# Output weights of an attention layer: both halves of a block made at once, differences written to memory instead of in place

## The chip, the cores and the metric

The kernel runs on one core of a Trainium2 chip. The metric is the time of one execution on the device in microseconds (us); lower is better. A core has a matrix engine (TensorE, "PE" in the profile, with its weight loads as "PEld"), a vector engine (VectorE, "DVE"), a scalar engine (ScalarE, "ACT"), GpSimd ("POOL") and SyncE ("SP"), which here issues all DMAs. Each engine works through its own queue in order and waits for the others by semaphores. Matmul results land in PSUM, in banks of 128 x 512 float32; only TensorE, VectorE and ScalarE work there. The other on-chip memory is SBUF.

## The reference, cut to what matters

Four residual blocks on x of shape 4 x 512 x 1024, each behind a layer norm: a small attention, a linear layer with routed low-rank additions, a causal attention with 32 heads over a compressed key/value of width 64, and a second linear layer with low-rank additions. The change lies in the causal attention, at its end:

```python
kv = _rmsnorm(ckv, kv_a_ln_w) @ wkv_b.T            # per head: 64 columns of keys, 128 of values
...
attn = jax.nn.softmax(scores, axis=-1)
out = jnp.einsum('bhqk,bkhd->bqhd', attn, v).reshape(B, S, H * VD)
return out @ wo.T
```

The kernel never makes v. A head's value weights (64 x 128) and its rows of `wo` (128 x 1024) are multiplied beforehand into a 64 x 1024 output weight; two heads make one 128 x 1024 block. The attention's result stays in the compressed form (64 numbers a head and token) and is multiplied by these blocks.

## The kernel before, in words

**Units.** The causal attention runs over 4 groups of 8 heads, and in each group over 4 batches: 128 units (group, batch, head), in the loop at L1215. In iteration u the kernel issues the scores of unit u (`scores`, four matmul groups of 512, 384, 256 and 128 columns into the two banks `pss`; VectorE masks each at L919, ScalarE takes the exponential at L922), the transposes of unit u-1 (`turn`, ten 128 x 128 transposes into the two banks `pst` at L943, copied at L945 by ScalarE twice and VectorE once), the context of units u-3 and u-2 together every second time (`context`, L959, the bank `psv`), and the query of unit u+3 (`query`, one bank `psq`, copied by ScalarE at L729, rotated by VectorE at L731 and L732 and by POOL at L733 and L734). `split_query` makes the high and the low part of a query for the scores: the cast `qh` on VectorE (L741), then the difference `ql` on POOL (L742).

Matmuls in full precision are three matmuls of split operands: each operand is a high part (a rounded copy) plus a low part (the difference to it). Lines L150, L151 and L152 (`matmul3`) carry these; their order is low x high, high x low, high x high, so `ql` is needed first. Transposes, contexts and the blocks below are single float32 matmuls.

**Fillers.** Between these, each iteration takes some steps from a generator, the filler, in three places; `per` (L1222) says how many in each. For most of the time the filler is `project`: the product of a batch's context with the group's output weights, seven products in place of eight for each 2 x 2 of blocks, into the banks `poa` and `pob`, added into x by VectorE (L1036). For the first batch of a group it is `prepare_output` (L1052): for group 0 over eight units, for groups 1 to 3 over the last four units of that batch. The order in which a scheduler then puts the instructions on each engine is fixed when the program is built; it may move a filler's instructions past those of the units around it.

**prepare_output.** Seven weights are wanted from a 2 x 2 of blocks, b11 and b12 (the halves, columns 0 to 511 and 512 to 1023, of one head pair), b21 and b22 (those of another): b11, b21 and b22 themselves, and t1 = b12 - b11, t2 = b22 - t1, t3 = b22 - b12, t4 = b21 - t2. A group has two such sets, and each of the 14 weights is kept as a high and a low part (tiles of the pool `wup`, one buffer each). `block` (L1063) makes one half of a block by two matmuls (L1069) into `poa` or `pob`, from `slotC`, the one buffer into which SyncE loads the weights of a head pair (L1047, L1049); after the second half the next pair is fetched. `kept` (L1077) copies a bank to `room`, six places of 128 x 512 in SBUF (named `raw` in the profile), on ScalarE. `high` (L1080) casts on ScalarE. `low` (L1086) subtracts on VectorE if its source is a bank, on POOL if it is a place of `room`. `less` (L1094) is a difference of two sources: on POOL if all is in `room`, otherwise on VectorE. Before, t1, t2 and t4 are made in the bank in which an operand stands, and t3 in `room` by POOL. One bank at a time is filled and worked off, so that 18 of the 32 half blocks stand alone among TensorE's instructions and 14 as pairs.

`kept`, `high`, `low` and `less` are 24 operations on ScalarE, 16 on VectorE and 6 on POOL in a group. VectorE's are held behind the last mask by `issue_after`.

## Time and profile before

| | |
|---|---|
| median of 3 runs | 1743.06 us (1740.99 to 1744.13) |
| the profiled execution | 1745.28 us |
| its span, first to last instruction | 1743.1 us |
| mean granted clock of TensorE | 0.998 |
| stages with output weights (us of the span) | 443 to 501, 739 to 776, 1010 to 1047, 1281 to 1318 |

The profile is of one execution. Busy times are sums over an engine's instructions; a busy TensorE is not TensorE at its peak, since the ends of pipelined matmuls are modelled. A row of a timeline has the start, the time from the first start to the last end of equal instructions in a row, the engine, the line, the operation with output<-input and shapes, the count, and in brackets the idle time before it with what ended it. A row of a group has minimum, median and maximum of one instruction in ns. A row of the waits has who waited for whom, the sum in us, how often, and the longest. The stages of groups 1 to 3 are alike; one of them in the table by stage:

```profile
739.00:776.00 37.00, 36.67 (x204) 23.55 (x200) 30.25 (x78) 29.76 (x78) 22.70 (x20) 1.00 0.59 194
```

Its columns are the stretch, its length, the busy time and count of PE, PEld, DVE, ACT and POOL, the granted clock, the share of the DMA engines and GB/s.

### The profile page before, as it was taken

Reading aid. Unit: us, or ns where it says so; the run is one execution under the profiler, and the core shown is the slowest. Engines: PE = TensorE matmul, PEld = TensorE weight load, DVE = VectorE, ACT = ScalarE, POOL = GpSimd, SP = SyncE. Lnnn points to the kernel's source line nnn. Section 1 sums busy time; section 2 is a strip of 40 time slices with the busy share of each in tenths; the row PEclk is TensorE's granted clock in tenths of the full one; section 3 lists DMA queues with packets and bytes.
Section 4 is the critical chain, followed back from the end, with each engine's and each line's share of the span. In section 5 each row is a group of like instructions: output and inputs, shape, how many; then the busy total and the mean of one; then the engine's idle time right before and its main releaser. Section 6 shows DMA issues by size and latency. Waiting matters only on the chain.

```text
span 1743.1 us, 31732 instructions
## 1 busy us (share of the span) xinstructions
PE 1703.5 (98%) x10536; PEld 1431.2 (82%) x10536; DVE 1305.5 (75%) x3494; ACT 902.6 (52%) x2316; POOL 925.4 (53%) x926
## 2 busy tenths in 40 slices
PE   7999999999999999999999999999999999999999
PEld 6899999998667877767787767777767777789998
DVE  7977885677877777787777777777778776687675
ACT  7422331366765555475555476555476555453332
POOL 0553541203666664666666656666566664575454
PEclk9999999999999999999999999999999999999999
DMA  4313543245324234353333353342454333853331
GB/s 195 134 40 118 181 164 114 89 139 164 115 87 150 81 109 150 104 176 114 110 122 113 105 201 97 105 140 95 133 168 151 103 111 120 303 196 122 138 117 62
DMA packets 131940, 228.17 MB, mean 131 GB/s; under 512 B 22272, under 2 KB 58752, under 8 KB 128448
## 3 DMA queue, kind: packets, MB, share of 16 engines
q1 hardware_dynamic: 131776, 226.13, 38.4%
q8 instruction: 84, 1.38, 0.3%
q14 instruction: 80, 0.66, 0.1%
HBM read 156.60 MB, written 71.83 MB: 131 GB/s over the span
## 4 chain that ended last, share of the span: by engine, by line
PE 85%; DVE 6%; DMA 3%; ACT 2%; issue 2%; POOL 2%; SPq 0%; ACTq 0%; DVEq 0%; POOLq 0%
PE psv L959 8%; PE pst L943 7%; PE po L150 4%; PE po L152 4%; PE po L151 4%; PE pss L150 4%; PE pss L151 4%; PE pss L152 3%; PE pob L150 3%; PE psq L150 3%; PE psq L151 3%; PE psq L152 3%; PE poa L150 3%; PE acc L150 3%; PE acc L152 3%; PE acc L151 3%
## 5 line engine op out<-in xcount | busy, mean ns | idle before, releaser
L922 ACT ACTIVATE p<-p,mn 128x512 f32<-128x512 f32 (+3 forms) x512 | 284.7, 558 | 218.0 <-DVE mn L919 217.6
L919 DVE CUSTOM_DVE_ANT_0 p<-pss,causal 128x512 f32<-128x512 f32 (+3 forms) x512 | 232.4, 486 | 27.4 <-PE pss L152 21.8
L733 POOL TENSOR_TENSOR qf<-qf,ropeT 64x512 f32<-64x512 f32 x128 | 164.6, 1286 | 166.4 <-ACT qf L729 163.4
L943 PE MATMUL pst<-ident,p 128*128 128x128 f32 x1280 | 186.4, 274 | 4.0 <-ACT pT L945 4.0
L734 POOL TENSOR_TENSOR qf<-qf,wA 64x512 f32<-64x512 f32 x128 | 164.4, 1285 | 29.9 <-DVE wA L732 23.4
L943 PEld LDWEIGHTS pst<-ident,p 128*128 128x128 f32 x1280 | 153.4, 141 | 31.4 <-ACT pT L945 8.7
L742 POOL TENSOR_TENSOR ql<-qf,qh 128x384 fp32r<-128x384 f32 x128 | 131.1, 1024 | 62.9 <-DVE qh L741 44.3
L994 POOL TENSOR_TENSOR cxl<-s,cxh 128x256 fp32r<-128x256 f32 x128 | 96.5, 762 | 120.6 <-ACT cxh L993 66.9
L945 ACT COPY pT<-pst 128x512 f32<-128x512 f32 x256 | 142.2, 577 | 23.2 <-PE pst L943 21.6
L150 PE MATMUL pss<-kT,ql 128*128 128x512 f32 (+2 forms) x384 | 142.8, 372 | 0.5 <-POOL ql L742 0.2
L150 PE MATMUL po<-w_h,hTl 128*128 128x384 f32 (+1 forms) x384 | 133.0, 346 | 0.5 <-DVE x L433 0.5
L151 PE MATMUL pss<-kT,qh 128*128 128x512 f32 (+2 forms) x384 | 130.9, 341 | 0.0
L152 PE MATMUL po<-w_h,hTh 128*128 128x384 f32 (+1 forms) x384 | 130.1, 339 | 0.0
L152 PE MATMUL pss<-kT,qh 128*128 128x512 f32 (+2 forms) x384 | 129.8, 338 | 0.0
L151 PE MATMUL po<-w_l,hTh 128*128 128x384 f32 (+1 forms) x384 | 129.7, 338 | 0.0
L945 DVE COPY pT<-pst 128x256 f32<-128x256 f32 x128 | 54.3, 424 | 94.2 <-PE pst L943 93.1
L729 ACT COPY qf<-psq 128x512 f32<-128x512 f32 x126 | 73.8, 586 | 71.9 <-PE psq L152 71.8
L731 DVE TENSOR_TENSOR wA<-psq,ropeT 32x512 f32<-32x512 f32 x126 | 87.7, 696 | 22.4 <-ACT qf L729 19.5
L994 POOL TENSOR_TENSOR cxl<-cx,cxh 128x256 fp32r<-128x256 f32 x96 | 73.5, 767 | 56.1 <-ACT cxh L993 53.5
L922 ACT ACTIVATION_READ_ACCUMULATOR p<-p,mn 128x1 f32 x512 | 97.0, 189 | 0.0
L150 PEld LDWEIGHTS pss<-kT,ql 128*128 128x128 f32 x384 | 72.1, 188 | 20.9 <-issue 3.6
L732 DVE TENSOR_TENSOR wA<-psq,ropeT 32x512 f32<-32x512 f32 x126 | 87.1, 691 | 1.7
(511 smaller groups left out, 4976.9 us busy)
## 6 DMA issues: line engine op xcount, KB each, us to landing
xs<-x_d SPq DMA_DIRECT2D x128, 256.0 KB
x_d<-xs SPq DMA_DIRECT2D x128, 256.0 KB
slotC<-in_woT_dram SPq DMA_DIRECT2D x32, 512.0 KB
rb<-r_d SPq DMA_DIRECT2D x128, 128.0 KB
w_t<-raw SPq DMA_DIRECT2D x32, 288.0 KB
x<-in_x_dram SPq DMA_DIRECT2D x16, 512.0 KB
x_d<-x SPq DMA_DIRECT2D x32, 256.0 KB
slotA<-q_d SPq DMA_DIRECT2D x8, 1024.0 KB
```

What stands on the lines that cost most here:

```text
L150: T.matmul(ps, lhsT=al, rhs=bh, start=start, stop=False, **kw)
L151: T.matmul(ps, lhsT=ah, rhs=bl, start=False, stop=False, **kw)
L152: T.matmul(ps, lhsT=ah, rhs=bh, start=False, stop=stop, **kw)
L733: G.tensor_tensor(f[mid], f[mid], ropeT[mid, 0, :], ALU.mult)
L734: G.tensor_tensor(f[mid], f[mid], t2[mid], ALU.add)
L742: G.tensor_tensor(l, f[:, P:S], f32(h), ALU.subtract)
L919: turn_of[0] = V.tensor_tensor_reduce(out=to, in0=ps[:, 0:n], in1=causal[:, S - n : S], scale=1.0, scalar=-NEG, op0=ALU.add, op1=ALU.min, ...
L922: A.activation(to, to, AF.Exp, bias=mn[:, i : i + 1], scale=-1.0, accum_out=rs[:, i : i + 1])
L943: T.transpose(ps[:, w : w + P], p[:, OF[i] + j * P : OF[i] + (j + 1) * P], ident)
L945: copy(pT[:, AT[js[0]] : AT[js[0]] + w], ps[:, 0:w])
L959: T.matmul(ps[n * KVR : (n + 1) * KVR, S - w : S], lhsT=k[:, j, :], rhs=pTs[u + n][:, AT[j] : AT[j] + w], start=(j == 0), stop=(j == TPB - 1))
L994: G.tensor_tensor(l, src, f32(h), ALU.subtract)
```

## The change

`block` now makes both halves, `poa` and `pob`, one right after the other, and fetches the next head pair behind them. Only b12 and b22 are copied to `room`; t1, t2, t3 and t4 are all made by VectorE from one operand in a bank and one in `room` (t3 from b22's bank and the kept b12), and written to places of `room`. So their high parts are cast from `room`, and their low parts, like that of b22, are made by POOL. A group has 18 operations on ScalarE, 12 on VectorE and 10 on POOL. There are 24 steps a group, the same for both sets, and `per` hands them out evenly: one in each of the three places for group 0, two in each for the other groups. The core of the diff:

```diff
-            def block(n, half, at):
+            def block(n):
                 nonlocal fetched
                 wo, wv = fetched
-                po[at] = pso.tile([P, 512], F32, name="po" + at)
                 with ExitStack() if g else tc.issue_after(scored[0].ins):
-                    for k in range(2):
-                        T.matmul(po[at][k * KVR : (k + 1) * KVR, :], lhsT=wv[:, k, :],
-                                 rhs=wo[k][:, half * 512 : half * 512 + 512], start=True, stop=True)
-                if half and n + 1 < len(prs):
+                    for half, at in enumerate("ab"):
+                        po[at] = pso.tile([P, 512], F32, name="po" + at)
+                        for k in range(2):
+                            T.matmul(po[at][k * KVR : (k + 1) * KVR, :], lhsT=wv[:, k, :],
+                                     rhs=wo[k][:, half * 512 : half * 512 + 512], start=True, stop=True)
+                if n + 1 < len(prs):
                     fetched = fetch_output(g, prs[n + 1])
...
             def less(to, a0, a1):
-                if not {to, a0, a1} & set(po):
+                if not {a0, a1} & set(po):
...
             def steps():
...
+                for n in (0, 2):
+                    block(n)
+                    if n:
+                        low("t4", 2)
+                    yield
+                    kept(1, "b")
+                    high("b11", "a")
+                    yield
+                    less(4, 1, "a")
+                    low("b11", "a")
+                    yield
+                    high("t1", 4)
+                    yield
+                    low("t1", 4)
+                    yield
+                    yield
+                    block(n + 1)
+                    yield
+                    kept(3, "b")
+                    high("b21", "a")
+                    less(5, "b", 4)
+                    yield
+                    high("b22", 3)
+                    low("b21", "a")
+                    less(2, "a", 5)
+                    less(0, "b", 1)
+                    yield
+                    high("t2", 5)
+                    low("b22", 3)
+                    yield
+                    high("t3", 0)
+                    low("t2", 5)
+                    yield
+                    high("t4", 2)
+                    low("t3", 0)
+                    if n:
+                        low("t4", 2)
+                    yield
...
-            per = ((4, 1, 0) if i % 2 else (1, 1, 0)) if b else (2 + (i < HG // 2 + 2), 2, 2) if i >= HG // 2 else (3, 3, 1)
+            per = ((4, 1, 0) if i % 2 else (1, 1, 0)) if b else (2, 2, 2) if i >= HG // 2 else (3, 3, 1)
             if B == 0:
-                per = (0, 1, 2)
+                per = (1, 1, 1)
```

The steps that went are the 22 written out one by one at L1101 to L1177.

More of the change, by code (lines that the diff above doesn't have):

```diff
@@ L1101, in steps @@
             def steps():
-                block(0, 0, "a")
-                yield
-                kept(0, "a")
-                high("b11", "a")
-                block(0, 1, "b")
-                yield
-                low("b11", "a")
-                kept(1, "b")
-                yield
-                less("b", "b", 0)
-                block(1, 0, "a")
-                yield
-                high("t1", "b")
-                kept(0, "b")
-                kept(2, "a")
-                high("b21", "a")
@@ L1118, in steps @@
-                yield
-                low("t1", "b")
-                low("b21", "a")
-                block(1, 1, "b")
-                yield
-                high("b22", "b")
-                kept(3, "b")
-                yield
-                low("b22", 3)
-                less("b", "b", 0)
-                block(2, 0, "a")
-                yield
-                high("t2", "b")
-                kept(5, "a")
-                less(3, 3, 1)
-                yield
-                low("t2", "b")
@@ L1135, in steps @@
-                less("b", 2, "b")
-                high("b11", "a")
-                yield
-                high("t4", "b")
-                high("t3", 3)
-                low("b11", "a")
-                yield
-                low("t4", "b")
-                low("t3", 3)
-                block(2, 1, "a")
-                yield
-                kept(1, "a")
-                yield
-                less("a", "a", 5)
-                block(3, 0, "b")
-                yield
-                high("t1", "a")
@@ L1152, in steps @@
-                kept(5, "a")
-                kept(2, "b")
-                high("b21", "b")
-                yield
-                low("t1", "a")
-                low("b21", "b")
-                block(3, 1, "a")
-                yield
-                high("b22", "a")
-                kept(3, "a")
-                yield
-                low("b22", 3)
-                less("a", "a", 5)
-                yield
-                high("t2", "a")
-                less(3, 3, 1)
-                yield
@@ L1169, in steps @@
-                low("t2", "a")
-                less("a", 2, "a")
-                high("t3", 3)
-                yield
-                high("t4", "a")
-                low("t3", 3)
-                yield
-                low("t4", "a")
-                yield
+                for n in (0, 2):
[36 more added lines that the diff above has]
+                    yield
```

## The prediction, made before the result was known

> **What bounds the kernel now.** I read the page first, then TensorE's waits, then the timelines of the four stretches in which the output weights are prepared (443 to 501 us for group 0; 739 to 776, 1010 to 1047 and 1281 to 1318 us for groups 1 to 3).

> ```profile
> PE 1703.5 (98%) x10536; PEld 1431.2 (82%) x10536; DVE 1305.5 (75%) x3494; ACT 902.6 (52%) x2316; POOL 925.4 (53%) x926
> ...
> PE 85%; DVE 6%; DMA 3%; ACT 2%; issue 2%; POOL 2%; SPq 0%; ACTq 0%; DVEq 0%; POOLq 0%
> ```

> TensorE is busy 98% of the span and holds 85% of the chain that ends last. So work taken from VectorE (DVE), ScalarE (ACT) or POOL is worth only what TensorE waits for it, and TensorE's own order counts. Over the whole span its second-largest wait is this one:

> ```profile
> PE pst L943 <- ACT pT L945: 4.0, 5, 2.2
> ```

> 2.2 of the 4.0 us are one wait near the end of group 0's preparation; three others of 0.49 us close the preparations of groups 1 to 3. The timeline shows what stands behind the long one:

> ```profile
> 487.82 0.39 PE L150 MATMUL pss<-kT,ql 128*128 128x512 f32 x1
> 490.46 0.44 PE L943 MATMUL pst<-ident,p 128*128 128x128 f32 x2 [2.25 <-ACT pT L945]
> ...
> 491.89 1.91 PE L943 MATMUL pst<-ident,p 128*128 128x128 f32 x8
> ...
> 502.59 1.04 PE L943 MATMUL pst<-ident,p 128*128 128x128 f32 x8
> ```
> ```profile
> 484.06 0.59 ACT L1083 CAST t21h<-poa 128x512 fp32r<-128x512 f32 x1 [1.51 <-DVE poa L1099]
> 487.13 0.62 ACT L1083 CAST t31h<-raw 128x512 fp32r<-128x512 f32 x1 [2.48 <-POOL raw L1096]
> ...
> 489.84 1.04 ACT L945 COPY pT<-pst 128x512 f32<-128x512 f32 x2
> ```
> ```profile
> 481.72 1.30 POOL L733 TENSOR_TENSOR qf<-qf,ropeT 64x512 f32<-64x512 f32 x1 [1.73 <-ACT qf L729]
> 483.09 1.28 POOL L1089 TENSOR_TENSOR b221l<-raw,b221h 128x512 fp32r<-128x512 f32 x1
> 484.45 1.28 POOL L734 TENSOR_TENSOR qf<-qf,wA 64x512 f32<-64x512 f32 x1
> 485.81 1.28 POOL L1096 TENSOR_TENSOR raw<-raw 128x512 f32<-128x512 f32 x1
> ```

> ScalarE stands still for t3, whose difference POOL makes (L1096). Behind the standing cast wait four exponentials and then the copies of the transposes (L945), and TensorE waits for these: 2.25 us. After it the eight transposes take 1.91 us where they normally take 1.04: the granted clock is 0.5 for one stretch of 3.41 us, from 491.5 (the 0.97 mean clock in the table by stage for 443 to 501). That costs about 1.7 us more.

> **The change part by part.**

> *Engine work.* Per group ScalarE loses 6 copies (24 in four groups, 0.48 us from start to start: 11.5 us), VectorE 4 operations (16, 0.60 us: 9.6 us), POOL gains 4 (16, 1.36 us from start to start by the rows above: 21.8 us). All of it lies beside TensorE's work: 0 by itself.

> *TensorE's blocks.* The matmuls are the same 64; only their neighbours change. A lone block, and a pair behind a context stage (psv):

> ```profile
> 445.74 0.39 PE L152 MATMUL psq<-slotA,wqh 128*128 128x512 f32 x1
> 446.06 1.08 PE L1069 MATMUL pob<-slotC 128*64 128x512 f32 x4
> 447.07 0.44 PE L943 MATMUL pst<-ident,p 128*128 128x128 f32 x2
> 447.26 0.48 PE L150 MATMUL pss<-kT,ql 128*128 128x512 f32 x1
> ...
> 1279.35 2.38 PE L959 MATMUL psv<-pT,slotA 128*64 128x512 f32 x16
> 1281.56 1.03 PE L1069 MATMUL poa<-slotC 128*64 128x512 f32 x4
> 1282.42 1.03 PE L1069 MATMUL pob<-slotC 128*64 128x512 f32 x4
> 1283.37 0.39 PE L150 MATMUL pss<-kT,ql 128*128 128x256 f32 x1
> ```

> From the psq row to the pss row it is 1.52 us with the block and 0.37 without it (459.92 to 460.29): 1.15. Other lone blocks come to 1.11 to 1.22; I take 1.17. Context stage and pair take 4.02 us; a context stage alone takes 2.30 (439.51 to 441.81): the pair costs 1.72. Before, 18 half blocks stand alone and 7 pairs together (pairs inside a context stage cost 1.7 to 1.9): 18 x 1.17 + 7 x 1.75 = 33.3. In the built order of the changed program there are 16 pairs: 10 behind a context stage (1.72) and 6 in the middle of other work, where each also pays about 0.1 on both sides (2.0): 29.2. **-4.1 us**; bounds -2.6 (lone blocks no dearer than 1.09) and -4.7.

> *Waits that go.* No high part waits for POOL any more. 2.25 + 1.7 + 3 x 0.49 = 5.4 us. Before, the second load of slotC arrived 0.23 and 0.29 us late in two groups, since only two steps lay between a fetch and its block; now there are six: 0.5. **-5.9 us.** Next in line ScalarE waits for VectorE's differences (0.6 us each, in the same queue as the masks); TensorE has transposes, a query and scores (3 us) to do before it needs ScalarE again, and that hides them. Without this cover it would be 0.6 a difference, at most 1.2 a place.

> *The burst on POOL.* Lows of t1, t2 and t4 move to POOL, and the built order puts them in a row: in group 0, after each second block, rotation L733, low t2, low t3, rotation L734, low t4, and only then the low part ql of the query that the next unit's scores need first. Nothing of before does this; there ql came right behind its own rotation. I add it up from the start of such a block, by rows of before:
> - TensorE: block 1.82, scores 0.46, last scores 0.22, eight transposes 0.80, query 1.48: 4.77. The result of the query is there at 5.03.
> - ScalarE copies it, POOL starts L733 0.72 us later: 5.75. Five operations at 1.36: ql starts at 12.55, ends (1.02) at 13.6.
> - TensorE meanwhile, from 4.77: two transposes 0.14, scores of 512 columns 0.78 (447.26 to 448.04), of 384 0.62, four transposes 0.44, one context matmul 0.43: 7.2. The next query waits for VectorE's rotation (L731, L732: ScalarE's copy, then two of 0.70 behind a difference) until 7.4. Query 1.5, four transposes and the short scores, with the waits for VectorE's masks between them, 2.9 in all: at 10.3 TensorE needs ql.

> A stall of 3.3 us, in two places of group 0. Nothing hides it. Bounds for one: 0 (if the scheduler's neighbours give POOL its copy 3.3 us earlier) and 4.7 (one more 1.36). As 2.25 us of idle time took half a clock stretch before, I add 1.7 each: 2 x 5.0 = **+10.0 us**.

> [...]

> *The same burst in groups 1 to 3.* Units there are longer (9 us for 7). Middle: ql is ready 12.4 us after the block's start, TensorE comes at 12.45: a tie. End: four lows stand between L733 and L734, so the cast of the next query (L741) holds VectorE until 9.4, the mask of the next scores ends at 12.05 and TensorE comes at 11.9; VectorE then runs about 0.4 late once more. I take 0.6 a group: **+1.8 us**; bounds 0, and 8.2 if each of the six places is one POOL operation (1.36) later. The table by source shows that the cast suffers from a busy POOL as it is:

> ```profile
> L741 DVE CAST qh<-qf x128: 310/362/740, 418.5 to 1462.2; 128x384 fp32r<-128x384 f32 x128
> ```

> [...]

> *Sum.* -4.1 - 5.9 + 10.0 + 1.8 = +1.8 us. The profiled execution took 1745.28 us (span 1743.1), 2.2 above the median of the runs, 1743.06. On the median: **1744.8 us**, no change that a measurement of this kernel can tell (about 0.2%, 3.5 us).

> **Rivals.**
> - *The burst is hidden* (the query's copy comes earlier, or TensorE later by work I did not see): only the gains stay, -10.0, or -8.2 with the ties: 1733 to 1735. For it: POOL is busy 37.5 of 58 us in group 0, so on average there is room. Against it: the order is fixed, and five times 1.36 behind one copy is more than the 5.3 us that TensorE has left.
> - *The burst also stalls groups 1 to 3* (the other side). Same mechanism: ql and the cast behind L734. Price 1.36 a place, six places: 8.2 in place of 1.8: 1751. It decides from 0.2 us of lateness on, since both places are ties. [...] Against it: groups 1 to 3 show 0.5 us or less of any such wait now.
> - *Half of the new stalls*: one of the two places hidden: 1740.
> - That the change does not do what it says is excluded: the built order shows 18, 12 and 10 operations a group.

> **How the numbers follow.** Forecast 0.50 (its own range 1740 to 1749: 0.05 faster, 0.37 same, 0.08 slower), burst hidden 0.17 (0.16 faster, 0.01 same), groups 1 to 3 too 0.25 (0.24 slower, 0.01 same), half 0.08 (0.05 faster, 0.03 same). Faster 0.26, same 0.42, slower 0.32. The range takes in most of both sides: 1733 to 1753.

> **What would show it.** Right: no wait of ScalarE for POOL; 16 pairs of blocks; TensorE waiting for "POOL ql L742" twice between 443 and 505 us, about 3 us each, with two clock stretches of 0.5; no waits above 0.5 us in groups 1 to 3. Wrong: ql on time (then about 1734), or waits for ql or for the mask in every group (then 1750 and more).

## The result, and the profile after

The changed kernel takes 1747.97 us (median of 7 runs, 1745.68 to 1754.8), the kernel before, beside it on the same chip, 1743.06 (7 runs, 1740.88 to 1744.55): a ratio of 1.0035, 95% interval 1.0023 to 1.0046. It is slower by 4.9 us. The forecast was 1744.8 in a range of 1733 to 1753. The time lies in the range, but beyond the bound of 0.2% within which the forecast called it no change. The profiled execution took 1746.9 us, its span is 1744.7. Of the executions below, one of run 6 (5862.85 us) and one of run 10 (2095.26 us) lie far above all others; the ratios leave them out, the medians count them.

The page's first line and its chain, after. TensorE is as busy as before, ScalarE 8.5 us less (11.5 reckoned), VectorE 7.1 less (9.6) and POOL 22.6 more (21.8); POOL's share of the chain has doubled (4% for 2%):

```profile
PE 1702.5 (98%) x10536; PEld 1433.1 (82%) x10536; DVE 1298.4 (74%) x3478; ACT 894.1 (51%) x2292; POOL 948.0 (54%) x942
...
PE 85%; DVE 5%; POOL 4%; ACT 3%; issue 2%; DMA 1%; SPq 0%; POOLq 0%; ACTq 0%; DVEq 0%
```

Two of TensorE's waits, after (who waited for whom, sum in us, times, longest). The first was 0.2 us before, the second 2.9, and the wait for ScalarE's copies (4.0) has shrunk to 0.3:

```profile
PE pss L150 <- POOL ql L742: 5.4, 3, 2.6
PE pob L150 <- POOL cxl L994: 4.9, 5, 1.6
```

TensorE's timeline has the two stalls at the two predicted places, 2.61 us each, and after the second one the rest of a context stage that takes 3.98 us for 14 records, at half clock (0.57 granted from 500 to 504 us, 0.50 from 500.09 to 503.50). (A float32 matmul of a context or a block stands in the profile as two records, so that a context stage of eight matmuls has 16.) The first row is the scores right behind the block of the first place:

```profile
455.67 0.39 PE L150 MATMUL pss<-kT,ql 128*128 128x256 f32 x1
...
464.49 0.38 PE L943 MATMUL pst<-ident,p 128*128 128x128 f32 x2
467.48 0.50 PE L150 MATMUL pss<-kT,ql 128*128 128x512 f32 x1 [2.61 <-POOL ql L742]
...
498.77 0.50 PE L150 MATMUL pss<-kT,ql 128*128 128x512 f32 x1 [2.61 <-POOL ql L742]
...
500.22 3.98 PE L959 MATMUL psv<-pT,slotB 128*64 128x512 f32 x14
```

POOL's timeline ahead of the first stall is the chain of the prediction (the difference of a low part is now L1090), without a break from 459.59 on. TensorE has its `ql` at 467.48, 11.81 us after the scores behind the block (455.67). Predicted were 13.6 from the block's start, 1.82 of them for the block, so 11.8 from there. The block itself is mixed with the last matmuls of a context here, from 453.21 on:

```profile
459.59 1.28 POOL L733 TENSOR_TENSOR qf<-qf,ropeT 64x512 f32<-64x512 f32 x1 [1.21 <-ACT qf L729]
460.96 1.28 POOL L1090 TENSOR_TENSOR t20l<-raw,t20h 128x512 fp32r<-128x512 f32 x1
462.19 1.41 POOL L1090 TENSOR_TENSOR t30l<-raw,t30h 128x512 fp32r<-128x512 f32 x1
463.68 1.28 POOL L734 TENSOR_TENSOR qf<-qf,wA 64x512 f32<-64x512 f32 x1
465.04 1.44 POOL L1090 TENSOR_TENSOR t40l<-raw,t40h 128x512 fp32r<-128x512 f32 x1
466.44 1.95 POOL L742 TENSOR_TENSOR ql<-qf,qh 128x384 fp32r<-128x384 f32 x2
```

One thing in TensorE's order was not reckoned with. Four of the five context stages in group 0's preparation now have their first matmul (two records) issued early and alone; from 446.99 to the next start it is 1.00 us, and as much at 460.59:

```profile
446.99 1.07 PE L959 MATMUL psv<-pT,slotA 128*64 128x512 f32 x2
447.99 0.38 PE L150 MATMUL pss<-kT,ql 128*128 128x256 f32 x1
```

Where the time went, by TensorE's starts: from the 512-column scores of unit 3 to those of unit 13 (group 0's preparation), and of units 38 to 50 (group 1's). A matmul's time is that to the next start; idle time over 0.06 us is kept apart.

```
units 3 to 13     blocks  contexts  queries  projection  scores, transposes  idle   total
before              7.49     14.38    14.96        5.16               31.30  2.25   75.53
after               8.04     15.94    15.27        5.12               30.51  5.44   80.31
units 38 to 50
before              7.25     15.04    17.77       22.31               35.66  1.00   99.04
after               8.24     14.89    17.46       21.93               35.50  1.02   99.04
```

Group 0 is 4.8 us longer; group 1 is equal to 0.01, group 2 0.24 longer, group 3 0.22 shorter. So between these two executions the change costs time in group 0 alone, and about as much as the medians differ (4.9). Each kernel has one profiled execution, and half clock falls otherwise in others (mean clocks from 0.995 to 1.000, last section). The two spans differ by only 1.6, since the execution profiled before had a half-clock stretch near its start (at 51.2 us; the later one was 1.88 us ahead at unit 0) and lost 1.4 more from the last unit's scores on; both are outside the stages that the change touches.

### The profile page after: what moved, and what is told of

It reads as the page before. It is cut to its first block, busy times and chain, and to the rows that moved or that the text cites. A ratio compares the mean times of both kernels' runs of the same rounds, so it can differ in the third digit from the quotient of the medians.

```text
span 1744.7 us, 31689 instructions
## 1 busy us (share of the span) xinstructions
PE 1702.5 (98%) x10536; PEld 1433.1 (82%) x10536; DVE 1298.4 (74%) x3478; ACT 894.1 (51%) x2292; POOL 948.0 (54%) x942
## 4 chain that ended last, share of the span: by engine, by line
PE 85%; DVE 5%; POOL 4%; ACT 3%; issue 2%; DMA 1%; SPq 0%; POOLq 0%; ACTq 0%; DVEq 0%
PE psv L959 8%; PE pst L943 7%; PE po L150 4%; PE po L152 4%; PE po L151 4%; PE pss L150 4%; PE pss L151 3%; PE pss L152 3%; PE pob L150 3%; PE poa L150 3%; PE psq L150 3%; PE psq L151 3%; PE psq L152 3%; PE pob L152 3%; PE pob L151 3%; PE acc L150 3%
## 5 line engine op out<-in xcount | busy, mean ns | idle before, releaser
L733 POOL TENSOR_TENSOR qf<-qf,ropeT 64x512 f32<-64x512 f32 x128 | 164.5, 1285 | 159.6 <-ACT qf L729 157.6
L943 PE MATMUL pst<-ident,p 128*128 128x128 f32 x1280 | 183.7, 273 | 0.3 <-ACT pT L945 0.3
L734 POOL TENSOR_TENSOR qf<-qf,wA 64x512 f32<-64x512 f32 x128 | 164.7, 1287 | 25.9 <-DVE wA L732 18.8
L943 PEld LDWEIGHTS pst<-ident,p 128*128 128x128 f32 x1280 | 152.2, 141 | 27.3 <-ACT pT L945 5.4
L742 POOL TENSOR_TENSOR ql<-qf,qh 128x384 fp32r<-128x384 f32 x128 | 131.7, 1030 | 61.1 <-DVE rt L884 24.6
L945 ACT COPY pT<-pst 128x512 f32<-128x512 f32 x256 | 141.8, 577 | 43.0 <-PE pst L943 42.0
L994 POOL TENSOR_TENSOR cxl<-s,cxh 128x256 fp32r<-128x256 f32 x128 | 96.9, 764 | 119.7 <-ACT cxh L993 68.4
L150 PE MATMUL pss<-kT,ql 128*128 128x512 f32 (+2 forms) x384 | 142.3, 370 | 6.0 <-POOL ql L742 5.4
L150 PE MATMUL po<-w_h,hTl 128*128 128x384 f32 (+1 forms) x384 | 132.9, 346 | 0.0
L152 PE MATMUL po<-w_h,hTh 128*128 128x384 f32 (+1 forms) x384 | 130.1, 339 | 0.0
L152 PE MATMUL pss<-kT,qh 128*128 128x512 f32 (+2 forms) x384 | 129.4, 337 | 0.0
L945 DVE COPY pT<-pst 128x256 f32<-128x256 f32 x128 | 54.2, 424 | 94.3 <-PE pst L943 93.6
L729 ACT COPY qf<-psq 128x512 f32<-128x512 f32 x126 | 73.5, 584 | 71.0 <-PE psq L152 70.7
L994 POOL TENSOR_TENSOR cxl<-cx,cxh 128x256 fp32r<-128x256 f32 x96 | 73.1, 763 | 58.2 <-ACT cxh L993 55.5
L731 DVE TENSOR_TENSOR wA<-psq,ropeT 32x512 f32<-32x512 f32 x126 | 87.7, 696 | 22.0 <-ACT qf L729 19.1
L150 PEld LDWEIGHTS pss<-kT,ql 128*128 128x128 f32 x384 | 72.2, 188 | 29.5 <-issue 7.3
L732 DVE TENSOR_TENSOR wA<-psq,ropeT 32x512 f32<-32x512 f32 x126 | 87.1, 691 | 1.7
```

The costliest lines, as they stand in the source:

```text
L150: T.matmul(ps, lhsT=al, rhs=bh, start=start, stop=False, **kw)
L152: T.matmul(ps, lhsT=ah, rhs=bh, start=False, stop=stop, **kw)
L733: G.tensor_tensor(f[mid], f[mid], ropeT[mid, 0, :], ALU.mult)
L734: G.tensor_tensor(f[mid], f[mid], t2[mid], ALU.add)
L742: G.tensor_tensor(l, f[:, P:S], f32(h), ALU.subtract)
L943: T.transpose(ps[:, w : w + P], p[:, OF[i] + j * P : OF[i] + (j + 1) * P], ident)
```

## The experiments

Theory 1 is the prediction's: the burst of low parts on POOL makes `ql` late in group 0, and that costs two stalls and clock. Theory 2, the rival: TensorE's new order costs the time, by the context matmuls that are issued alone. Theory 3: half-clock stretches that fall by chance. Ten kernels were run, each timed against the kernel before, which had medians of 1743.1, 1742.9 and 1742.7 us in the three sets.

**1. `ql` ahead of the low parts.** `split_query` keeps its difference, and `low` queues POOL's low parts behind it; TensorE's, VectorE's and ScalarE's orders are unchanged:

```diff
-        G.tensor_tensor(l, f[:, P:S], f32(h), ALU.subtract)
+        split_of[0] = G.tensor_tensor(l, f[:, P:S], f32(h), ALU.subtract)
...
-                    G.tensor_tensor(l, src(at), f32(h), ALU.subtract)
+                    with tc.issue_after(split_of[0].ins):
+                        G.tensor_tensor(l, src(at), f32(h), ALU.subtract)
```

> The changed kernel with the low parts on POOL queued behind the query's low part (ql) that was split last; TensorE's, VectorE's and ScalarE's orders are those of the changed kernel, instruction by instruction. Theory 1 (the burst on POOL makes ql late): both waits of 2.61 us for ql in group 0 go, with the clock stretch (1.7 us) that one of them took: 5.2 to 6.9 us less than the changed kernel, 1741 to 1743. Theory 2 (the new order of TensorE costs the time: context stages whose first two matmuls are issued alone, about 1.0 us each): its order is unchanged, so the time stays at 1747 to 1748. Theory 3 (the difference is clock stretches that fall by chance in the runs): no difference from the changed kernel outside the interval.

Measured: 1743.23 us, 4.7 less than the changed kernel; against before 1.000 (0.9991 to 1.0008). First POOL, then TensorE at the same place: `ql` now goes ahead of the low parts, and TensorE passes from the transposes to the scores without a wait.

```profile
461.52 1.27 POOL L734 TENSOR_TENSOR qf<-qf,wA 64x512 f32<-64x512 f32 x1 [0.22 <-DVE wA L732]
463.16 1.00 POOL L742 TENSOR_TENSOR ql<-qf,qh 128x384 fp32r<-128x384 f32 x1 [0.36 <-DVE qh L741]
464.12 1.30 POOL L1093 TENSOR_TENSOR b220l<-raw,b220h 128x512 fp32r<-128x512 f32 x1
```
```profile
465.06 0.38 PE L945 MATMUL pst<-ident,p 128*128 128x128 f32 x2
465.19 0.48 PE L150 MATMUL pss<-kT,ql 128*128 128x512 f32 x1
```

Group 0 takes 74.06 us in place of 80.31: the burst cost 6.25. The stalls (5.2) and the half clock behind the second (contexts 14.33 for 15.94) are gone, and 1.0 of smaller waits has come. Theory 1 holds for the difference between the kernels; theories 2 and 3 would have left the time where it was.

**2. A longer burst** (b22's low part three times in group 0):

```diff
-                    G.tensor_tensor(l, src(at), f32(h), ALU.subtract)
+                    for _ in range(3 if g == 0 and kind == "b22" else 1):
+                        G.tensor_tensor(l, src(at), f32(h), ALU.subtract)
```

> The changed kernel with the low part of b22 in group 0 made three times instead of once, so that two more POOL operations (2.6 us) stand ahead of each of the two bursts; all other engines have the same order. POOL stands still for 1.21 us there, so its chain is 1.4 us later. Theory 1: each of the two waits for ql grows from 2.6 to 4.0 us: 2.8 us more than the changed kernel, 4.5 if the longer idle time takes one more clock stretch: 1750.5 to 1752.5. Theories 2 and 3: no change (1747 to 1748).

Measured: 1754.36 us, 6.4 more than the changed kernel, above what theory 1 expected. Each stall is 3.83 us, 1.22 longer (1.4 expected), and now both are followed by half clock (0.57 granted from 470 to 474 us and from 504 to 508). The matmul behind the first:

```profile
470.12 0.68 PE L150 MATMUL pss<-kT,ql 128*128 128x512 f32 x1 [3.83 <-POOL ql L742]
```

In the traces group 0 grows by 4.4: 2.9 of idle time, 2.4 of it in the two stalls, and 1.4 of clock. The two profiled executions differ by 5.7 in all, 1.2 of it ahead of unit 0. So the cost follows the length of the burst, as theory 1 has it; theories 2 and 3 had no change.

**3. Context stages in one piece**, in all groups; `last_of[0]` is the last matmul of the latest scores that have their low parts, those of 384 columns when a context is issued:

```diff
+            with tc.issue_after(last_of[0].ins):
+                for j in range(TPB):
...
+                        T.matmul(ps[n * KVR : (n + 1) * KVR, S - w : S], lhsT=k[:, j, :],
```

> The changed kernel with each context stage queued behind the scores of 384 columns of its own iteration, so that no first pair of context matmuls is issued alone; in the new order 7 pairs of blocks stand behind a context stage and 9 behind a query, where 10 and 6 stood behind a context stage and behind scores. Theory 2: four split stages in group 0 and two to three in each of the other groups give back about 1.0 us each, 10 to 12 us, less 3 x 0.3 for the pairs that no longer follow a context stage: 1737 to 1739. Theory 1: in group 0 TensorE only comes earlier to the same late ql, so that half of what is saved there is given back in the two waits (about 3.6 us each instead of 2.6): 2 us less gain, 1739 to 1741, with both waits for ql still there and longer. Theory 3: no difference.

Measured: 1754.3 us, 6.3 more than the changed kernel, where no theory expected more time. Theory 2 falls as it was stated. In group 0 the context matmuls go down (13.45 us for 15.94), but both waits for `ql` stay (2.82 and 2.71 us), each is followed by half clock, and the first half-clock stretch is a double one (the context stage behind it, 16 records in one piece, takes 4.26 us). In groups 1 to 3 the edit did not do what it was meant to: no first matmul is alone, but two stages a group are now split elsewhere, around transposes, and in units 38 to 50 contexts take what they took (14.87 us for 14.89) and TensorE's own time is no less (98.42 for 98.02). So this run does not test theory 2 there. Idle time grows in each of these groups (1.75, 1.75 and 2.92 us for 1.02, 1.02 and 0.82). One of these two stages:

```profile
756.55 2.15 PE L961 MATMUL psv<-pT,slotA 128*64 128x512 f32 x10
758.63 0.66 PE L944 MATMUL pst<-ident,p 128*128 128x128 f32 x4
759.22 0.86 PE L961 MATMUL psv<-pT,slotA 128*64 128x256 f32 x6
```

**4. Both edits.**

> Both edits together: context stages in one piece, and the low parts on POOL behind the query's low part. Theories 1 and 2 together: no wait for ql, no lone pairs: 1747.5 - 6 - 10 = 1731 to 1734, faster than the kernel before. Theory 1 alone: as the first of these runs, 1741 to 1743. Theory 2 alone: as the third, 1737 to 1739.

Measured: 1746.24 us; 1.0016 (1.0008 to 1.0025), outside all three expectations. With both edits group 0 is 1.2 us shorter than in the first run (72.85 for 74.06), and groups 1 to 3 are 0.9, 0.9 and 2.4 longer. TensorE's waits in this run:

```profile
PE pob L150 <- DVE xs L1040: 3.6, 4, 1.3
...
PE pst L946 <- ACT pT L948: 2.3, 4, 0.7
```

The projection waits for VectorE's sums, and the transposes for ScalarE's copies. It looks as if the lone matmuls had filled time in which these were made; that was not tried by itself, and in groups 1 to 3 two stages are split around transposes as in run 3.

**5. The kernel before, with ScalarE's cast of t3 behind the exponentials.** Nothing of the change is in it:

```diff
-                A.copy(h, src(at))
+                with tc.issue_after(exp_of[0].ins) if kind == "t3" else ExitStack():
+                    A.copy(h, src(at))
```

> The kernel before with one edit: ScalarE's cast of t3 is queued behind the exponentials of its iteration, so that ScalarE no longer stands still for POOL's difference in front of them. Nothing of the change itself is in it. If the prediction's term for the wait that goes is right (2.25 us, a clock stretch of 1.7, 0.49 in each of three groups), 5.4 us less than before: 1737 to 1739. If the wait is filled by the next one in line (VectorE's differences, or ql), 1741 to 1743.

Measured: 1737.98 us; 0.9972 (0.9963 to 0.9981). ScalarE's copies of the transposes come in time, and the cast stands behind them:

```profile
487.62 0.57 ACT L946 COPY pT<-pst 128x512 f32<-128x512 f32 x1
488.13 0.59 ACT L729 COPY qf<-psq 128x512 f32<-128x512 f32 x1
488.62 0.62 ACT L1085 CAST t31h<-raw 128x512 fp32r<-128x512 f32 x1
```

4.9 us of the 5.4 expected are there. In group 0 it is 4.3 (71.22 us for 75.53). Idle time is 1.7 of it (0.51 for 2.25), and the 3.41 us at half clock are worth another 1.7. The remaining 0.9 is about what run 6 gives for a context stage in one piece (0.8): one that was split there before (at 493.73) is whole now. VectorE's and POOL's built orders have shifted a little with the edit too. Groups 1 to 3 change by -0.3, +0.1 and -0.3, where 1.5 was reckoned: their waits for ScalarE, 0.5 at most, are still there. This kernel beats both.

**6. The first run's kernel, with the contexts of group 0 alone in one piece** (the `issue_after` of run 3 under `if g == 0`).

> The first experiment's kernel (low parts on POOL behind ql) with the context stages of group 0 alone kept in one piece; those of the other groups stay as in the changed kernel, and so do all pairs of blocks. If a context stage whose first two matmuls are issued alone costs about 0.5 us (2.1 us between the first and the fourth run in group 0, for four stages), 2 us less than the first run's 1743.2: 1741. If what was gained there came from the shifted pairs of blocks instead, no change (1743).

Measured: 1742.14 us; 0.9995 (0.9986 to 1.0004), 1.1 less than the first run. The contexts of group 0 take 11.12 us in place of 14.33, 0.8 less for each of the four stages, which are whole now:

```profile
452.61 2.38 PE L963 MATMUL psv<-pT,slotA 128*64 128x512 f32 x16
```

But the idle time rises from 1.23 to 3.01 (waits for masks, for VectorE's sums and for ScalarE), and the stage is 1.2 shorter, about half of what was expected.

**7. The low parts of the last t3 and t4 of groups 1 to 3 on VectorE**, the rest as in the first run:

```diff
+                    if g and len(wouts[g][kind]) == 2 and kind in ("t3", "t4",):
+                        with tc.issue_after(turn_of[0].ins):
+                            V.tensor_tensor(l, src(at), f32(h), ALU.subtract)
+                        return
```

> The first experiment's kernel with the low parts of the last t3 and t4 of groups 1 to 3 on VectorE instead of POOL, two POOL operations less in the burst of four at the end of each of these stages. If that burst is what makes TensorE wait for the projection's low part (L994) at the stage's end, 1.02, 1.01 and 0.82 us in the three groups, these go: 2 to 2.8 us less than 1743.2: 1740.5 to 1741.2. If VectorE's two more operations delay masks by as much, no change.

Measured: 1745.09 us; 1.0015 (1.0006 to 1.0024), 1.9 more than the first run, which neither side expected. At the stages' ends the waits for the projection's low part shrink from 1.02, 1.01 and 0.82 us to 0.2 or nothing, and waits for masks come (0.7, 0.7 and 1.5). The whole execution's rows for these two:

```profile
PE pss L150 <- DVE mn L921: 3.4, 6, 0.8
...
PE pob L150 <- POOL cxl L996: 2.0, 2, 1.6
```

So whichever of POOL and VectorE gets the operations is late. But that is not the whole of the loss: in groups 1 and 2 idle time is as before the edit (1.09 and 1.07 us for 1.02 and 1.01), and the stages are 1.1 and 0.9 longer by TensorE's own contexts, queries and projection, whose order has changed too.

**8. The halves of a block in different steps again**, the rest as in the first run: `block(n, 1)`, a step, `block(n, 0)`, with the work on a bank behind its own half.

> The first experiment's kernel with the two halves of a block made in different steps again; in its order 12 half blocks stand alone, the others in pairs or fours, where the changed kernel has 16 pairs. By the prediction's prices (1.17 us a lone half, 1.72 to 2.0 a pair) 12 x 1.17 + 10 x 1.75 + 0.7 = 32.2 in place of 29.2: 3 us more, 1746. If a half block costs the same alone as in a pair, as the sums over a stage of the kernel before and of the first run say (blocks, contexts, queries and projection of units 38 to 50: 62.4 us before, 62.5 after), no change: 1743.

Measured: 1751.06 us; 1.0045 (1.0032 to 1.0059). Slower by 7.8 than the first run, and above both expected numbers. In units 38 to 50 blocks, contexts, queries and projection take 7.10 + 16.04 + 17.44 + 21.92 = 62.50 us, where the first run has 8.17 + 14.96 + 17.46 + 21.93 = 62.52, and the kernel before, with its 18 lone halves in all, 62.37. The masks are late:

```profile
PE pss L150 <- DVE mn L921: 4.3, 2, 3.3
PE pss L915 <- DVE mn L921: 3.2, 4, 1.0
```

In the new steps one has four operations of VectorE; that these are what delays the masks is read from the order and was not tried. The longest of the waits, 3.28 us, is followed by half clock too (the two 384-column matmuls that come next take 0.53 us each, those at 438.88 in the trace before 0.34 and 0.35). The disputed price of a half block is not settled by the equal sums: the three kernels split their context stages in different places (blocks 8.17 and contexts 14.96 us in the first run, 7.10 and 16.04 here), and a split costs about as much as the price in question (0.8 us, run 6).

**9. Run 5 with all context stages in one piece.**

> The fifth experiment's kernel (the kernel before, ScalarE's cast of t3 behind the exponentials) with every context stage in one piece too. Three context stages there, one in each of groups 1 to 3, have their first two matmuls issued alone. If these cost 0.5 to 0.8 us each and nothing takes their place, 1.5 to 2.4 us less than 1738.0: 1736. If the wait for copies or masks takes their place, as in the third experiment's groups 1 to 3 (1 to 2 us a group more), 1738 to 1742.

Measured: 1738.0 us; 0.9974 (0.9964 to 0.9984), the same as run 5. Group 0 is 1.0 shorter. In groups 1 to 3 contexts lose 1.3 us each, and a wait of 1.5 for the low part of t4 comes in their place.

**10. One part of the change undone, in group 0 alone: the low parts of t2, t3 and t4 on VectorE.**

```diff
+                    if g == 0 and kind in ("t2", "t3", "t4"):
+                        with tc.issue_after(turn_of[0].ins):
+                            V.tensor_tensor(l, src(at), f32(h), ALU.subtract)
+                        return
```

> The changed kernel with one part of the change undone in group 0 alone: the low parts of t2, t3 and t4 are made by VectorE (held behind the last mask) instead of POOL. Theory 1 (POOL's burst): both waits for ql go with the clock stretch, 1741 to 1743, as in the first experiment. If VectorE's three more operations (0.6 us each) make a mask late by what is taken from POOL, a wait for masks takes their place: 1745 and more.

Measured: 1743.25 us; 1.0004 (0.9995 to 1.0013). No wait for `ql` and no half clock in group 0 (the mean clock of the profiled execution is 1.000); what comes in place is one wait of 1.2 us for VectorE's copy and 0.8 of smaller ones. Two different ways of taking the burst off POOL's path (1 and 10) give the same time.

## Why the prediction was in the range and on the wrong side of no change

The way from before to after in group 0 falls into three steps by the traces: wait removed -4.3 (before to run 5), new order of the engines +2.8 (run 5 to run 1), burst +6.3 (run 1 to after), together +4.8. They add up by construction; what is measured is the size of each. Groups 1 to 3 give 0.0. Against the prediction's terms:

```
term                              predicted   measured
waits that go                       -5.9        -4.3 (group 0), -2.0 (groups 1 to 3)
burst on POOL, group 0             +10.0        +6.3
next waits in groups 1 to 3         +1.8        +2.0
blocks, TensorE's order             -4.1        +2.8 (group 0), 0.0 (groups 1 to 3)
sum                                 +1.8        +4.8
```

- **Waits that go.** Right. 2.25 of stall and 1.7 of clock were expected in group 0; run 5 has 4.3 there, 1.7 of idle time, 1.7 of clock and 0.9 that is probably a context stage. In groups 1 to 3 the waits for ScalarE and for slotC are gone: idle time there was 1.00, 0.80 and 1.07 us before, of which 0.28, 0.31 and 0.29 the wait for the projection's low part (L994), and the difference, 2.0, is gone.
- **The burst.** Mechanism and places were right (runs 1, 2 and 10), and POOL's chain to 0.1 us in the time at which `ql` is ready. The size was 6.3 in place of 10.0. TensorE needed `ql` 9.2 us after the end of the block (at 464.87), not 8.5, mostly since the context matmul that goes early and alone took 1.0 us where 0.43 was reckoned: a stall of 2.6 instead of 3.3. And in the profiled execution one of the two stalls took a clock stretch, not both; the two lie differently in the grid of 3.413 us that the traces have (below), and the single case of 2.25 us could not tell that.
- **Ties in groups 1 to 3.** The amount was near, which is luck, since the place was not. No wait for `ql` or for masks came there. The four low parts in a row on POOL delay the projection's low part instead, whose wait is now 1.02, 1.02 and 0.82 us, 2.0 more than before, where the prediction had no wait above 0.5 as a sign of being right. Run 7 shows how near VectorE is: freed from two low parts, POOL is on time and the masks are late.
- **Blocks on TensorE.** This is the term that failed, in its sign. The prediction took a context stage as one piece of 2.30 us, though the built order has four split ones in group 0, each with 0.8 us more of TensorE's time (runs 4 and 6): 3.2 us that the sum does not have. Of the +2.8, 2.1 are TensorE's own time (72.82 us in run 1 for 70.71 in run 5) and 0.7 idle time (1.23 for 0.51). In one piece the contexts give only 1.2 of the span (run 6), since waits for VectorE and ScalarE fill the rest. Whether the prices in the term, 1.17 for a lone half and 1.72 to 2.0 for a pair, are right is open. In units 38 to 50 blocks, contexts, queries and projection take 62.52 us after for 62.37 before (0.18 and 0.24 more in the other two groups, scores and transposes as much less), where these prices ask for 0.7 less a group; but the changed kernel has two split context stages there and the kernel before one, and a split of 0.8 hides as much. In group 0, runs 6 and 9 have no context matmul alone: TensorE's own time is 69.83 us with pairs and 70.11 with lone halves, 0.3 less, where the prices ask for 1.9.

So a gain of 4 us that was a loss of 3 stood against a loss that was 4 us too large: the number came out only 3 us too low because two errors partly cancelled, and that it lies in the range owes something to luck. The rival "burst hidden" is excluded by the two stalls, and its price was wrong as well: with the burst off the path the kernel is at 1743.2, as before, not at 1733 to 1735, because the new order gives back most of what the removed wait had gained. The rival of six stalls (1751) is excluded by groups 1 to 3, which have no wait for `ql`, and that of a single stall (1740) by the second one.

## What to carry to other kernels

Moving work to an engine with room on average is priced by the queue: write down which operation of the critical path stands behind the moved ones in program order, and when it is due. Where only the order is wrong, change the order: one `issue_after` on a cast in the kernel before gave 4.9 us, the wait that the rewritten stage removes at the price of new ones. And price TensorE's order by the sum over a whole stage in two kernels, not by rows of single groups, since the cost of a pattern shows up in its neighbours' rows; then list what else was moved between the two, here the splits of the context stages, before the difference is put down to one pattern.

## What the runs showed of the hardware

```
          idle in a window, us                            next window
before    2.25 (from 488.11 on), 1.92 (from 47.79 on)     0.5
after     2.09 (from 496.68 on)                           0.5
run 2     3.26, 3.41                                      0.5
run 3     2.37, 2.71                                      0.5
run 3     0.45 (rest of a stall, in a window at 0.5)      0.5
run 8     2.99                                            0.5
before    1.62 and less, all others from 20 to 1739 us    1.0
after     1.62 and less, all others from 20 to 1739 us    1.0
```

No window of the traces before and after has between 1.62 and 1.92 us. The changed kernel's two stalls of 2.61 us are the example: the second lies with 2.09 us in one window and is followed by half clock, the first is cut by an edge (465.96) into 1.2 and 1.5 (the grid's sums) and is not. So of these two stalls of one length one cost 1.6 us more (contexts 15.94 us, 14.33 in run 1). The seven executions of the changed kernel, 1745.7 to 1754.8 us, have mean clocks from 1.000 (the shortest) to 0.995 (the longest). One stretch takes 0.001 from the mean clock of a span (half of 3.41 in 1743). Of 68 executions of the kernel before, timed beside the experiments, 21 have 1.000 (mean time 1742.1 us) and 17 have 0.998 (1744.1). So at least 21 had no such stretch, and what a stall costs differs from one execution to the next.

**A float32 context matmul issued alone took 1.0 us** (stationary 128 x 64, 512 columns, two records; after, 446.99 to 447.99), while the eight of a whole stage, of 512 to 128 columns, took 2.30 in a row (before, 439.51 to 441.81). By the stage sums of runs 1 and 6 a stage split in this way costs TensorE 0.8 us more, and the span less (1.2 for four).

**VectorE's cast beside a busy POOL** ran up to 1.36 us (before: 0.74), median 0.38. In the trace after, the 42 casts during which POOL did nothing took 0.31 to 0.36 us, the other 86 took 0.33 to 1.36; in the trace before, 51 took 0.31 to 0.36 and the other 77 0.35 to 0.74. The five over 1.0 us (at 461.4, 492.7, 757.6, 1028.9 and 1300.3) all lie in the stages with output weights, each across two low parts on POOL that follow one another:

```profile
L741 DVE CAST qh<-qf x128: 308/378/1356, 416.6 to 1465.2; 128x384 fp32r<-128x384 f32 x128
```
